# One change to a five-layer attention kernel on one core: keys placed by transfers into kept block-diagonal tiles

## The chip, the core and the metric

The kernel runs on one core of a Trainium2 chip. A core has five engines that run their own instruction streams and wait for each other by semaphores: PE (TensorE, matrix products; PEld is its weight load), DVE (VectorE), ACT (ScalarE), POOL (GpSimd) and SP (SyncE), whose queue here only issues DMA transfers. PE writes its results to PSUM, all other data lie in SBUF, both with 128 partitions. The metric is the device time of one execution in microseconds. A profile is one execution recorded instruction by instruction.

## The reference, cut

The input x has 128 batches of 64 tokens with 128 channels; ctx is a second such tensor and cond one row of 128 channels per batch. Five residual blocks with attention follow each other, then a mixture of experts. All is float32. One attention with 16 heads of 8 channels, as the first block has it:

```python
mod = silu(t_emb) @ adaln_w + adaln_b
sh_sa, sc_sa, g_sa, sh_ff, sc_ff, g_ff = split(mod, 6)
xm = _ln(x) * (1.0 + sc_sa) + sh_sa
q, k, v = heads(xm @ qkv_w + qkv_b)              # 16 heads of 8
attn = softmax(einsum('bhnd,bhsd->bhns', q, k) * 8 ** -0.5)
x = x + g_sa * (einsum('bhns,bhsd->bhnd', attn, v) @ sa_proj_w + sa_proj_b)
```

The order is: layer L0 with self-attention (L0s), cross-attention to ctx (L0c) and an MLP; L1 with cross-attention (L1c); L2 with self-attention (L2s), cross-attention (L2c) and an MLP; L3 with a gated mixture of three experts.

## The kernel before

The tokens are cut into 16 groups of 512 (8 batches), kept in SBUF as xs[s], four tiles of 128 tokens by 128 channels. Each attention layer runs over the 16 groups; a group in a layer is called a unit here, 80 in all, 32 in the first run (L0s, L0c) and 48 in the second (L1c, L2s, L2c). The order of all instructions is written out by hand; nothing is rescheduled. Each engine executes its own in that order, and SP takes its transfers in that order too: one whose condition isn't met holds up all behind it.

A unit passes through three generators.

- prepare (L378) has eight stages: load ctx (c, L386); statistics of x (L312, L314, then POOL's L321, L322); the normalized xn (L364); transposes and modulation into kv_in and q_in; keys kT (PE L428, ACT L430) and from them kbd (L436); queries qT (L441, L443); values (L451) into vbd (L456, L457).
- scores, turned and weighted (L460 to L520) work on a half of a unit (4 batches): PE computes the scores sc (L470) into the only PSUM tile of that kind, DVE takes the maximum mx (L477) and the difference e (L479), PE transposes it (pp, L495), ACT takes the exponential (eT, L499), PE multiplies by vbd (po, L512), ACT copies to o (L520).
- finish (L522) has four stages: sums of the weights leave o for DRAM, come back as rc, and half of o's rows are moved (L530, L534, L537); reciprocal (L539), out as recs, gates gt in self layers (L278), and recs spread back over the partitions as rb (L541, L546); oT = o times rb on POOL (L549); projection py (L555) and the addition to x.

kbd is the block-diagonal form of the keys: partition p holds channel p; for each j of 4 there is a copy in which only channels of heads 4g + j are not zero, so that one product of 32 rows gives the scores of four heads apart. Before, POOL makes the four copies by multiplying kT with a column of a mask of ones and zeros.

vbd holds, for a pair of heads, the values in columns 0 to 7 and 8 to 15, and columns of ones at 16 and 17 that give the softmax's sums. The product po therefore has in each block of 32 rows 16 rows of results and two rows of sums, and o has two such halves; finish moves the second half's rows 0 to 15 to rows 16 to 31 of the first.

attend (L563) interleaves: step k handles a half of unit i. In the first half of unit i it calls, after the scores, one transposition and weighted, in this order: finish of unit i-2 (its stage with recs, gt and rb), prepare of unit i+4 (its first: the load of c), prepare of unit i+1 (its kT and kbd), finish of unit i-3 (projection). In the second half stand prepare of i+1 (queries, then values) and finish of unit i-1 (sums, rc, o) and of i-2 (oT). mlp runs over the groups between the layers, layer_3 at the end; both begin with the same statistics.

Of the kernel before, what the change touches and what calls it, by code (L numbers as in the profile page):

```python
# [35 lines left out]
for _name, _n in _VECS:  # L36
# [14 lines left out]
    "L3_xcond_gate_w1": (3, 128), "L3_xcond_gate_w2": (1, 128), "L3_xcond_out_w": (1, 128),  # L51
}
_RAW = [
    "x", "cond_1024", "ctx_1024", *_WTS,
# [5 lines left out]
def tile_kernel(ctx: ExitStack, tc: tile.TileContext, a: dict, out: bass.AP):  # L60
# [17 lines left out]
    nc.scalar.dma_start(vec_rows, a["vecs"])  # L78
    mask = const([P, 4], "mask")
    nc.scalar.dma_start(mask, a["mask"])  # L80

    w = {}

    def load_weights(prefix, pool=cp):
        for name, (k, n) in _WTS.items():
            if name.startswith(prefix):
                t = pool.tile([P, k, n], F32, tag=name, name=name)
                src = a[name]
                if len(src.shape) == 3:
                    src = src.rearrange("e c n -> (e c) n")  # L90
                nc.sync.dma_start(t, src.rearrange("(k p) n -> p k n", p=P))
                w[name] = t
# [26 lines left out]
    ident = const([P, P], "ident")  # L119
    make_identity(nc, ident)  # L120
    nhalf = const([P, TT], "nhalf")
    G.memset(nhalf, -0.5)
# [45 lines left out]
    ]  # L168

    def clear(t):  # L170
        G.memset(t, 0.0)
        G.memset(t[0:L, :, :, 16:17], 1.0)
        G.memset(t[L:P, :, :, 17:18], 1.0)
# [5 lines left out]
    scT = const([P, P], "scT")  # L179
    mods = {}  # L180

    def col(name, i=0):
        r = _ROW[name] + i
        return vec[:, r : r + 1]
# [20 lines left out]
    def folded_column(wp, bp, bv, i):  # L205
        pb = mm("pb")
        T.matmul(pb[:, 0:1], w[wp][:, 0], col(bv, i), start=True, stop=True)
        t = const([P, 1], "pb_" + wp)
        V.tensor_add(t, pb[:, 0:1], col(bp))
        proj_bias[wp] = t  # L210
# [3 lines left out]
    def gate_table(wmod, wp, i=2, bias=None):  # L214

        table = dp.tile([P, 2, P], F32, tag="gate_" + wp, name="gate_" + wp)
        rows = const([P, 2, P], "gate_rows")
        gb = const([P, P], "gate_bias")
        V.tensor_scalar_mul(gb, mods[wmod][:, i, :], proj_bias[wp] if bias is None else bias)

        def second():
            pg = mm("pg")
            for q, src in enumerate((mods[wmod][:, i, :], gb)):
                T.transpose(pg[:, ts(q, P)], src, ident)
            V.tensor_copy(rows, pg[:, 0 : 2 * P].rearrange("p (i c) -> p i c", i=2))
            nc.sync.dma_start(table, rows)
            gates[wp] = table

        return second

    def folded_row(wp, bp, bv):
        bvs = const([P, P], "bvs")
        V.tensor_copy(bvs, col(bv, 1).broadcast_to([P, P]))

        def second():
            pb = mm("pb")
            T.matmul(pb[:, :P], bvs, w[wp][:, 0], start=True, stop=True)
            V.tensor_add(row_bias[bp], row_bias[bp], pb[:, :P])
            proj_bias[wp] = row_bias[bp]

        return second

    def condition():
        pc = mm("pc")
        T.transpose(pc[:, :P], cond, ident)
        V.tensor_copy(condT, pc[:, :P])
        S.activation(scT, pc[:, :P], AF.Silu)
        pv = mm("pv")
        T.transpose(pv[:, :_NVEC], vec_rows, ident[:_NVEC, :_NVEC])
        V.tensor_copy(vec, pv[:, :_NVEC])  # L250
        V.tensor_scalar_add(vec1, vec, 1.0)

# [20 lines left out]
    def gate_tile(pool, s, wp):  # L273

        gt = pool.tile([P, TT, 2, P], F32, tag="gt", name="gt")
        for h in range(2):
            r = gates[wp].rearrange("(s t h) i c -> s h t (i c)", t=TT, h=2)[s, h]
            nc.sync.dma_start(  # L278
                gt[ts(h, L)].rearrange("p t i c -> p t (i c)"),
                r.unsqueeze(0).broadcast_to([L, TT, 2 * P]),  # L280
            )
        return gt
# [23 lines left out]

    x_mv = const([P, NST, TT, 2], "x_mv")

    def stats(pool, src, mv):
        st = pool.tile([P, TT, 6], F32, tag="st", name="st")  # L310
        for t in range(TT):
            V.bn_stats(st[:, t, :], src[:, t, :])  # L312
        for t in range(TT):
            V.bn_aggr(mv[:, t, :], st[:, t, :])  # L314

# [4 lines left out]
    def power(rs, mv, eps):  # L320
        G.tensor_scalar(rs, mv[:, :, 1], eps, 1.0, ALU.add, ALU.mult)  # L321
        G.tensor_tensor(rs, rs, nhalf, ALU.pow)  # L322
        return rs

    def stats_of(pool, src, eps):
        mv = pool.tile([P, TT, 2], F32, tag="mv", name="mv")
        stats(pool, src, mv)
        return mv, inv_std(pool, mv, eps)
# [30 lines left out]
    def normed_by_pool(pool, src, mv, rs, tag, engine=G):  # L359
        nmu = pool.tile([P, TT], F32, tag="nmu" + tag, name="nmu")  # L360
        G.tensor_scalar(nmu, mv[:, :, 0], -1.0, 0.0, ALU.mult, ALU.add)
        xn = pool.tile([P, TT, P], F32, tag=tag, name=tag)
        for t in range(TT):
            engine.tensor_scalar(  # L364
                xn[:, t, :], src[:, t, :], nmu[:, t : t + 1], rs[:, t : t + 1], ALU.add, ALU.mult
            )
        return xn
# [5 lines left out]

    turn = [0]

    ctxT = dp.tile([NST, P, NT], F32, tag="ctxT", name="ctxT")

    def prepare(pools, at):  # L378
# [54 lines left out]
        vbd = vbds[i]  # L433
        kbd = pool.tile([P, 4, NB, L], F32, tag="kbd", name="kbd")
        for j in range(4):
            (V if at.get("first") else G).tensor_scalar(  # L436
                kbd[:, j], by_batch(kT), mask[:, j : j + 1], 1.0, ALU.mult, ALU.mult
            )
        yield
# [15 lines left out]
        pv4 = pvv.rearrange("p b (i d) -> p b i d", d=HD)  # L455
        S.copy(vbd[0:L, :, :, 0:HD], pv4[0:L])  # L456
        S.copy(vbd[L:P, :, :, HD : 2 * HD], pv4[L:P])  # L457
        at["vbd"] = vbd
# [63 lines left out]
    def finish(pools, at):  # L522
# [5 lines left out]
        sums = dp.tile([16, NT], F32, tag="sums", name="sums", bufs=2)  # L528
        for j in range(2):
            nc.sync.dma_start(  # L530
                sums.rearrange("(g i j) t -> j g i t", i=2, j=2)[j], o[16 + j : P : 32, :, :]
            )
        rc = pool.tile([P, L], F32, tag="rc", name="rc")
        nc.sync.dma_start(rc, sums.rearrange("h (c t) -> (h c) t", t=L))  # L534

        for g in range(4):
            nc.sync.dma_start(o[32 * g + 16 : 32 * g + 32, 0, :], o[32 * g : 32 * g + 16, 1, :])  # L537
        yield
# [6 lines left out]
        rb = pool.tile([P, NT], F32, tag="rb", name="rb", bufs=1)  # L545
        nc.sync.dma_start(rb, recs.unsqueeze(1).broadcast_to([16, HD, NT]))  # L546
        yield
# [69 lines left out]
    def attention_of(s, layer):  # L617
        if layer[2] == "s":
            wmod, wqkv, bqkv, wp = {
                "L0s": ("L0_xcond_adaln_w", "L0_xcond_qkv_w", "L0_xcond_qkv_b", "L0_xcond_sa_proj_w"),  # L620
                "L2s": ("L2_xcond_W_mod", "L2_xcond_W_qkv", "L2_xcond_b_qkv", "L2_xcond_W_proj"),
            }[layer]
            m = w[wqkv][:, 0]
            return dict(
                s=s, layer=layer, wmod=wmod, wp=wp, wq=m[:, 0:P], bq=col(bqkv, 0),
                wk=m[:, P : 2 * P], bk=col(bqkv, 1), wv=m[:, 2 * P : 3 * P],
            )
# [12 lines left out]
        return dict(  # L640
            s=s, layer=layer, wp=wp, wq=w[wq][:, 0], bq=col(bq), wk=m[:, 0:P], bk=col(bkv, 0),
            wv=m[:, P : 2 * P],
# [12 lines left out]
    def measure_context(s):  # L655
        pool = pools[0]
        mv = pool.tile([P, TT, 2], F32, tag="mvc", name="mvc")
        stats(pool, measured[s], mv)
        load_context(s + 2)
        nmu = pool.tile([P, TT], F32, tag="nmuc", name="nmuc")  # L660
        G.tensor_scalar(nmu, mv[:, :, 0], -1.0, 0.0, ALU.mult, ALU.add)
        rs = ctx_rs[:, s]
        for i, eps in enumerate(ctx_eps):
            G.tensor_scalar(rs[:, i], mv[:, :, 1], eps, 1.0, ALU.add, ALU.mult)
        G.tensor_tensor(rs, rs, nhalf.unsqueeze(1).broadcast_to([P, 2, TT]), ALU.pow)
        G.tensor_tensor(ctx_nb[:, s], nmu.unsqueeze(1).broadcast_to([P, 2, TT]), rs, ALU.mult)

    def mlp(wmod, w1, b1, w2, b2, beside, mv_out=None, by_token=False):
# [52 lines left out]
        def leave(d):  # L721
# [4 lines left out]
            if mv_out is not None:  # L726
                stats(pool, xs[d["s"]], mv_out[:, d["s"]])

# [453 lines left out]
    def stages():  # L1182
# [42 lines left out]
        ahead_1(0, 1, 2, 3)  # L1225
        condition()
        ahead_1(0, 0)
        first_mods[0]()
# [14 lines left out]
        n = last + 2 + len(heads_0)  # L1243
        for f in steps_1[6:-n]:
            f()
        for s in range(2):
            heads_0[3 + s] = lambda s=s, f=heads_0[3 + s]: (f(), load_context(s))
# [69 lines left out]
```

## Time and profile before

| what | before |
|---|---|
| median of 3 runs | 1629.09 us (1629.08 to 1633.11) |
| profiled execution, span | 1629.3 us |
| mean granted clock of PE | 0.995 |
| first run of 32 attention units | up to about 400 us |
| MLP of L0 | about 400 to 550 us |
| second run of 48 attention units | about 550 to 1130 us |
| MLP of L2, then L3 | about 1130 to 1629 us |
| POOL on kbd (L436) | 212.7 us, 316 instructions, mean 692 ns |
| DVE on statistics (L312, of x) | 110.5 us, 512 instructions, mean 278 ns |
| DVE on L314 (into mv) | 40.4 us, 448 instructions, mean 152 ns |
| DVE on mx and e (L477, L479) | 366.5 and 366.6 us, 160 each, mean 2291 ns |
| transfers on SP's queue | 108.53 MB, 25.8% of 16 engines |

The page gives each engine's busy time, then the chain: the work that ended last, followed back step by step to what released it. An engine with much idle time that is rarely on the chain can be made lighter or heavier without changing the span, as long as no wait grows out of it. In the chain and the timelines a row starts with its start and its duration in us; "x32" means 32 instructions run together. SPq is SP's queue issuing a transfer; the duration there is that of the issue, not of the transfer.

### The profile page before, as it was taken

What the parts mean: (1) busy time and instruction counts of PE and PEld (TensorE: products, weight loads), DVE (VectorE), ACT (ScalarE), POOL (GpSimd) and SP (SyncE); (2) the same over time, 40 slices, a digit from 0 to 9 for tenths busy, and PEclk for the clock granted to TensorE, in tenths of its full rate; (3) what the DMA queues carried; (4) which work ended last, traced back from release to release, by engine and by line L of the source; (5) the groups of instructions that cost most, each with busy time, mean ns of one, the idle gap of its engine ahead of it and who ended that gap; (6) DMA issues with size and microseconds to landing.
All of it is one profiled execution on the core that took longest, in us unless ns stands there. A gap on an engine that the chain in (4) does not pass through costs nothing.

```text
span 1629.3 us, 64936 instructions
## 1 busy us (share of the span) xinstructions
PE 1578.3 (97%) x27842; PEld 1090.4 (67%) x27842; DVE 1295.3 (79%) x2430; ACT 1036.9 (64%) x1710; POOL 1074.1 (66%) x1786
## 2 busy tenths in 40 slices
PE   6999999998999899999999999998999999999998
PEld 4677767776544467767777777776777666666665
DVE  7999989999566688899999999997454567666666
ACT  5788767776433687787888888886334544444443
POOL 6678776775888789987778877665876333333322
PEclk9999999999999999999999999999999999999999
DMA  7334443322112022211333532222433111111100
GB/s 209 83 82 98 107 119 87 94 80 74 49 33 63 16 60 62 61 52 45 89 91 82 123 90 61 74 56 60 118 91 78 30 40 36 40 33 35 34 11 20
DMA packets 146782, 112.71 MB, mean 69 GB/s; under 512 B 36357, under 2 KB 125247, under 8 KB 146495
## 3 DMA queue, kind: packets, MB, share of 16 engines
q1 hardware_dynamic: 146288, 108.53, 25.8%
q8 instruction: 219, 3.59, 0.9%
q14 instruction: 68, 0.56, 0.1%
q10 hardware_dynamic: 207, 0.03, 0.0%
HBM read 83.99 MB, written 14.02 MB: 60 GB/s over the span
## 4 chain that ended last, share of the span: by engine, by line
PE 80%; DVE 12%; ACT 3%; POOL 2%; DMA 1%; issue 1%; SPq 0%; POOLq 0%; DVEq 0%
PE sc L470 9%; PE pp L495 8%; PE ph L685 7%; PE po L512 7%; PE ph L1072 6%; PE ph L1073 6%; DVE mx L477 5%; DVE e L479 5%; PE po L1103 5%; PE psT L334 5%; PE pk L428 4%; PE py L555 4%; PE py L701 4%; PE py L691 3%; PE pq L441 3%; PE pvv L451 3%
## 5 line engine op out<-in xcount | busy, mean ns | idle before, releaser
L499 ACT ACTIVATE eT<-pp 128x1024 f32<-128x1024 f32 x320 | 329.8, 1031 | 163.2 <-PE pp L495 163.0
L477 DVE TENSOR_REDUCE mx<-sc 128x32 f32<-128x2048 f32 x160 | 366.5, 2291 | 60.2 <-PE sc L470 60.2
L479 DVE TENSOR_TENSOR e<-sc,mx 128x2048 f32<-128x2048 f32 x160 | 366.6, 2291 | 5.4
L495 PEld LDWEIGHTS pp<-ident,e 64*128 64x128 f32 x5120 | 184.9, 139 | 141.0 <-ACT eT L499 45.3
L495 PE MATMUL pp<-ident,e 64*128 64x64 f32 x5120 | 228.7, 229 | 7.1 <-DVE e L479 4.7
L436 POOL TENSOR_SCALAR kbd<-kT,mask 128x512 f32<-128x512 f32 x316 | 212.7, 692 | 30.8 <-ACT kT L430 28.3
L364 POOL TENSOR_SCALAR xn<-x,nmu,rs 128x128 f32<-128x128 f32 x508 | 223.9, 456 | 13.3
L549 POOL TENSOR_TENSOR oT<-o,rb 128x512 f32<-128x512 f32 x80 | 102.1, 1277 | 162.8 <-DMA rb<-recs 60.1
L470 PE MATMUL sc<-kbd,qT 32*64 32x256 f32 x5120 | 181.0, 390 | 17.0 <-DVE e L479 15.2
L686 ACT ACTIVATE h<-ph,vec 128x512 f32<-128x512 f32 x128 | 87.4, 688 | 150.1 <-PE ph L685 149.9
L512 PE MATMUL po<-eT,vbd 128*32 128x64 f32 x10240 | 178.9, 222 | 0.9 <-issue 0.8
L1079 ACT ACTIVATE h<-h 128x512 f32<-128x512 f32 x112 | 70.6, 630 | 148.1 <-DVE h L1075 129.2
L512 PEld LDWEIGHTS po<-eT,vbd 128*32 128x32 f32 x10240 | 152.4, 110 | 13.7 <-DVE st L312 1.5
L322 POOL TENSOR_TENSOR rs<-rs,nhalf 128x4 f32<-128x4 f32 x128 | 130.3, 1018 | 10.7
L470 PEld LDWEIGHTS sc<-kbd,qT 32*64 32x64 f32 x5120 | 98.1, 132 | 53.9 <-issue 19.6
L1075 DVE TENSOR_TENSOR h<-ph,ab 128x512 f32<-128x512 f32 x112 | 76.9, 687 | 56.3 <-PE ph L1073 56.2
L312 DVE BATCH_NORM_STATS2 st<-x 128x6 f32<-128x128 f32 x512 | 110.5, 278 | 0.6
L1108 DVE SCALAR_TENSOR_TENSOR acc<-po,pr,acc 128x128 f32<-128x128 f32 x192 | 67.2, 350 | 44.1 <-PE po L1103 39.6
L1072 PE MATMUL ph<-nx,w 128*128 128x512 f32 x192 | 99.9, 602 | 0.0
L520 ACT COPY o<-po 128x512 f32<-128x512 f32 x160 | 95.7, 598 | 5.5 <-PE po L512 4.1
L1073 PE MATMUL ph<-u,w_ev 128*128 128x512 f32 x192 | 98.0, 592 | 0.0
L1103 PEld LDWEIGHTS po<-w_2o,h 128*128 128x128 f32 x768 | 92.1, 192 | 8.7 <-issue 8.4
(261 smaller groups left out, 2841.2 us busy)
## 6 DMA issues: line engine op xcount, KB each, us to landing
rb<-recs SPq DMA_DIRECT2D x80, 256.0 KB
c<-in_ctx_dram SPq DMA_DIRECT2D x64, 256.0 KB
o<-o SPq DMA_DIRECT2D x320, 32.0 KB
gt<-gate_L_xcond_sa_proj_w SPq DMA_DIRECT2D x32, 256.0 KB
gt<-gate_L_xcond_W_proj SPq DMA_DIRECT2D x32, 256.0 KB
gt<-gate_L_xcond_W_mlp SPq DMA_DIRECT2D x32, 256.0 KB
x<-in_x_dram SPq DMA_DIRECT2D x16, 256.0 KB
ctxT<-cm SPq DMA_DIRECT2D x16, 256.0 KB
```

What stands on the lines that cost most here:

```text
L322: G.tensor_tensor(rs, rs, nhalf, ALU.pow)
L364: engine.tensor_scalar(xn[:, t, :], src[:, t, :], nmu[:, t : t + 1], rs[:, t : t + 1], ALU.add, ALU.mult)
L436: (V if at.get("first") else G).tensor_scalar(kbd[:, j], by_batch(kT), mask[:, j : j + 1], 1.0, ALU.mult, ALU.mult)
L470: T.matmul(sc[ts(h, L), g, ts(t2, 256)], qT[ts(g, 32), ts(b, L)], kbd[ts(g, 32), :, b, :], start=True, stop=True,)
L477: V.tensor_reduce(mx, sc.rearrange("p g (m k) -> p (g m) k", k=L), AX.X, ALU.max)
L479: V.tensor_tensor(e, sc.rearrange("p g (m k) -> p (g m) k", k=L), mx.unsqueeze(2).broadcast_to([P, 32, L]), ALU.subtract,)
L495: T.transpose(pp[:, h, ts(4 * g2 + 2 * i + t2, L)], e6[ts(h, L), 2 * gg + g2, t2, i], ident[ts(h, L), ts(h, L)],)
L499: S.activation(eT[:, gg], pp, AF.Exp, scale=HD ** -0.5)
L512: T.matmul(po[ts(g, 32), i, ts(2 * t2 + h, L)], at["vbd"][:, 4 * u + 2 * t2 + h, 2 * g + i, :], e7[:, g // 2, h, g % 2, i, t2, :], start=T ...
L1072: T.matmul(ps, wn, d["nx"], start=True, stop=False)
L1073: T.matmul(ps, we, d["u"], start=False, stop=True)
L1103: T.matmul(po[:, ex, :], d[q][:, ts(t, P)], k3["w_2o"][:, q, :], start=r == 0, stop=r == 1)
```

## The change

Five parts belong together.

1. kbd becomes two kept tiles, kbds[0] and kbds[1], used in turn. The first two units still fill theirs by the mask, which writes the zeros. From the third on, four transfers on SP's queue (spread) copy 32 rows of 2 KB each from kT to the rows of kbd that aren't zero. For that, the rows of one j have to be p = j, j + 4, ...: the channels of q and k are put in the order (g d j), by reordering the columns of the weights once (reorder; the first on DVE at the start, the others on POOL in the first run) and the biases (vecp).
2. vbd writes the values into even columns; the sums' columns are 1 and 17. All results of po then lie in even rows. One transfer moves the second half into the odd rows (before four), one takes the sums out (before two). rb is filled by two transfers (before one). Projection weights are loaded in that row order, two transfers each, and the value biases follow (vecv).
3. The gates table is stored so that one transfer with rows of 4 KB loads a unit's gates (before two with rows of 1 KB).
4. Statistics take two tiles per call, interleaved, so that the even and odd results of bn_stats are those of the two tiles; bn_aggr goes, and POOL divides the sum of squares by 128.
5. The mask comes from the identity by one DVE reduction, not from DRAM.

```diff
+    kbds = [
+        Places.ak.tile([P, 4, NB, L], F32, tag=f"kbd{i}", name=f"kbd{i}", bufs=1) for i in range(2)
+    ]
     def clear(t):
         G.memset(t, 0.0)
-        G.memset(t[0:L, :, :, 16:17], 1.0)
+        G.memset(t[0:L, :, :, 1:2], 1.0)
         G.memset(t[L:P, :, :, 17:18], 1.0)
...
+    def reorder(engine, name, n):
+        for i in range(n):
+            t = const([P, P], "gate_bias")
+            cols = w[name][:, 0, ts(i, P)]
+            engine.tensor_copy(t.rearrange("p (g d j) -> p g d j", d=HD, j=4), by_element(cols))
+            engine.tensor_copy(cols, t)
...
+        r = gates[wp].rearrange("(s h t) i c -> s h (t i c)", t=TT, h=2)[s]
+        nc.sync.dma_start(
+            gt.rearrange("p t i c -> p (t i c)"),
+            r.unsqueeze(1).broadcast_to([2, L, TT * 2 * P]),
+        )
...
-        for t in range(TT):
-            V.bn_stats(st[:, t, :], src[:, t, :])
-        for t in range(TT):
-            V.bn_aggr(mv[:, t, :], st[:, t, :])
+    def stats(src, mv):
+        for i in range(2):
+            V.bn_stats(mv[:, i, :], src[:, ts(i, 2), :].rearrange("p t c -> p c t"))
...
-        G.tensor_scalar(rs, mv[:, :, 1], eps, 1.0, ALU.add, ALU.mult)
+        G.tensor_scalar(rs, squares(mv), 1.0 / P, eps, ALU.mult, ALU.add)
...
+    def spread(kbd, kT):
+        for j in range(4):
+            nc.sync.dma_start(kbd[j:P:4, j].rearrange("p b l -> p (b l)"), kT[j:P:4, :])
...
-        kbd = pool.tile([P, 4, NB, L], F32, tag="kbd", name="kbd")
-        for j in range(4):
-            (V if at.get("first") else G).tensor_scalar(
-                kbd[:, j], by_batch(kT), mask[:, j : j + 1], 1.0, ALU.mult, ALU.mult
-            )
+        kbd = kbds[i]
+        if turn[0] <= 2:
+            for j in range(4):
+                (V if at.get("first") else G).tensor_scalar(
+                    kbd[:, j], by_batch(kT), mask[:, j : j + 1], 1.0, ALU.mult, ALU.mult
+                )
+        else:
+            spread(kbd, kT)
...
-        S.copy(vbd[0:L, :, :, 0:HD], pv4[0:L])
-        S.copy(vbd[L:P, :, :, HD : 2 * HD], pv4[L:P])
+        S.copy(vbd[0:L, :, :, 0 : 2 * HD : 2], pv4[0:L])
+        S.copy(vbd[L:P, :, :, 2 * HD : 4 * HD : 2], pv4[L:P])
...
-        for j in range(2):
-            nc.sync.dma_start(
-                sums.rearrange("(g i j) t -> j g i t", i=2, j=2)[j], o[16 + j : P : 32, :, :]
-            )
+        nc.sync.dma_start(sums.rearrange("(m i) t -> m i t", i=2), o[1:P:16, :, :])
...
-        for g in range(4):
-            nc.sync.dma_start(o[32 * g + 16 : 32 * g + 32, 0, :], o[32 * g : 32 * g + 16, 1, :])
+        nc.sync.dma_start(o[1:P:2, 0, :], o[0:P:2, 1, :])
...
-        nc.sync.dma_start(rb, recs.unsqueeze(1).broadcast_to([16, HD, NT]))
+        for i in range(2):
+            r = recs.rearrange("(m i) t -> i m t", i=2)[i]
+            nc.sync.dma_start(rb[i:P:2, :], r.unsqueeze(1).broadcast_to([8, HD, NT]))
...
+        reorder(V, "L0_xcond_qkv_w", 2)
```

The last line stands in stages before the first unit's statistics.

## Prediction

> **What bounds the kernel now.** I read the page's busy times, its chain, then one steady period of the chain, the timeline of the same microseconds, and last SP's own rows.
>
> ```profile
> PE 1578.3 (97%) x27842; PEld 1090.4 (67%) x27842; DVE 1295.3 (79%) x2430; ACT 1036.9 (64%) x1710; POOL 1074.1 (66%) x1786
> ...
> PE 80%; DVE 12%; ACT 3%; POOL 2%; DMA 1%; issue 1%; SPq 0%; POOLq 0%; DVEq 0%
> ```
>
> PE is nearly always busy and carries 80% of the chain. POOL, which the change relieves, carries 2%. One attention unit (16 per layer, five layers, 80 in all) in layer L2s:
>
> ```profile
> 792.98 1.12 PE sc L470 x32
> 794.10 0.64 PE pp L495 x16
> 794.74 1.03 PE po L512 x64
> 795.77 1.05 PE pk L428 x2
> 796.83 0.92 PE py L555 x8
> 797.74 0.64 PE pp L495 x16
> 798.38 0.59 PE psT L334 x4
> 798.97 1.13 PE sc L470 x32
> 800.10 0.02 issue
> 800.13 2.30 DVE mx L477
> 802.43 0.02 issue
> 802.45 2.30 DVE e L479
> ```
>
> A unit is two halves. In the first PE alone is full (5.99 us from score to score); in the second sc, mx, e follow one another through the single PSUM tile (5.92 us). Together 11.92 us, and 12.01 in L0c and L2c, 12.27 in L1c (starts of mx in the timelines). There is no slack that a lighter POOL or DVE could use.
>
> ```profile
> 798.53 2.70 POOL L436 TENSOR_SCALAR kbd<-kT,mask 128x512 f32<-128x512 f32 x4
> 798.73 0.54 DVE L539 RECIPROCAL rc<-rc 128x64 f32<-128x64 f32 x1
> ...
> 799.30 0.33 SPq L541 DMA_DIRECT2D recs<-rc  x1
> ```
>
> This is the place to watch. POOL finishes kbd of the next unit at 801.23; its first scores run at 804.89, so today 3.7 us are spare. In the changed kernel those keys are moved by four DMAs that stand in SP's queue behind recs, (gt), rb and (c). SP waits in order, so they inherit every wait ahead of them.
>
> ```profile
> 653.50 0.33 SPq L541 DMA_DIRECT2D recs<-rc  x1
> 655.00 0.56 SPq L546 DMA_DIRECT2D rb<-recs  x1
> 655.61 0.58 SPq L386 DMA_DIRECT2D c<-in_ctx_dram  x1
> ```
>
> rb cannot issue before recs has landed: 1.50 us after recs was issued. Prices of a transfer between SBUF rows, and of a landing:
>
> ```profile
> L537 SPq DMA_DIRECT2D o<-o x320: 507/587/1974, 46.2 to 1145.0; - x160
> ...
> L534 SPq EVENT_SEMAPHORE  x80: 17/1297/2703, 44.5 to 1141.4; - x80
> ```
>
> The issue of an o row move takes 0.59 us of SP; SP then waits 1.30 us (median) for sums to land. The trace's semaphore events give the landing after the end of the issue: o rows 1.37 us, recs 1.14, rb 3.32, c 3.88 (medians).
>
> **The change part by part.**
>
> *Removed from POOL and DVE.* 78 units lose 4 x 0.691 us on POOL (216 us). Statistics go from 4 x 0.276 + 4 x 0.149 = 1.70 us to two calls of twice the length, about 2 x 0.5. In the period above bn_stats sits in DVE's wait for sc (792.75 to 793.9), in layer 3 PE is 100% busy between 1300 and 1400 us. Worth 0. Weight reorders on POOL are 16 copies of about 0.46 us (the xn row), 7 us, hidden by what POOL gives up. If DVE's or POOL's cover were the bound after all, the gain would be some 0.7 us a unit; that is rival 4.
>
> *ACT and the loads.* vbd's copies write every second element. Nearest row: 0.58 us each, plain. If that doubled (bound: 1.2 us more a unit), ACT, busy 151 of 185 us between 725 and 910, has 2.2 us a unit left, and vbd is read only a half later: 0. The five projection weights load in two transfers each; SP's loads end at 33.9 us now, so about 36.5. Behind them stand the first keys, of the third unit: 36.5 + 2.5 + 1.4 = 40.4, before its scores (mx at 44.6): 0.
>
> *SP's count.* A self unit had sums 2, rc, o 4, recs, gt 2, rb = 11 issues; now sums, rc, o, recs, gt, rb 2, keys 4 = 11. Sums, o and gt save 0.6 + 1.9 + 0.65 us of issue, but sums, rc and o stand behind the keys, after the point that matters. gt falls into the wait for recs. So nothing saved helps the keys, while rb's second issue delays them.
>
> *The new loop.* First scores of unit i, mx, e, reciprocal (DVE takes it after e), recs, rb, keys of i+1, first scores of i+1. Steps, in us:
> 1. scores' start to recs' issue: 799.30 - 792.98 = 6.32.
> 2. recs to rb: 1.50.
> 3. two rb issues at 0.56 + 0.04 = 1.20 (a half-sized one, bounds 0.33 to 0.56, taken like the whole). In cross layers also c, 0.62.
> 4. four keys at 0.59 + 0.04: 2.52. They are 32 rows of 2 KB; nearest row the o move, 16 rows of 2 KB, 0.59. Bounds 0.33 (recs, 128 rows of 256 B) and 0.71 (mean of the o moves).
> 5. landing of the last. Empty queues: 1.37. But rb and c fill the same engines: rb2 ends its issue at 2.70 and lands 3.32 later, 6.0; c ends at 3.3 and lands at 7.2. Keys issued last at 5.22 (self) land at 6.6 to 6.8, at 5.84 (cross) at 7.2 to 7.7. I take 6.7 and 7.5 counted from recs; bounds 6.6 and 8.3 (means in place of medians).
> 6. 0.1 for the semaphore.
>
> Medians: self 6.32 + 6.7 + 0.1 = 13.1, cross 13.9. Now the tails: of the o moves one in four lands later than 2.15 and one in ten issues longer than 1.25. Such hold-ups of about 1.5 us come every 10 us or so in the events between 787 and 850 us, and a loop without slack meets one in about half its turns: +0.7. So 13.8 and 14.6.
>
> The loop closes where a unit has both a finishing one two before it and one after it: i = 2 to 30 of the first 32 units, 2 to 46 of the other 48, 74 turns. By what stands ahead of the keys:
> - 20 with gt alone (self): 13.8 - 11.92 = 1.9, 38 us.
> - 12 with gt and c: 14.7 - 12.0 = 2.7, 32 us.
> - 20 with c in L0c and L2c: 14.6 - 12.01 = 2.6, 52 us.
> - 10 with c in L1c: 14.6 - 12.27 = 2.3, 23 us.
> - 12 with neither: 13.7 - 12.0 = 1.7, 20 us.
> Sum 165 us. While PE waits there, nothing behind sc can run on it: pp, po, pk, py of the same half all queue behind, and ACT and POOL wait for those.
>
> *Start.* DVE now reorders the first q and k weights before the first statistics. By the semaphore events those weights land at 6.4 us; statistics began at 4.38. Four copies at 0.29 (the condT copy) and 0.2 for waits end at about 7.8, two statistics at 8.8 instead of 5.53, and the chain of the start runs through them: +3.
>
> Profiled execution 1629.3 + 165 + 3 = 1797; the median of the runs is 1629.09, so nothing is to be added.
>
> [...]
> [...]
>
> ```profile
> 403.20:405.50 2.30, 0.01 (x2) 0.04 (x2) 2.14 (x1) 1.02 (x1) 0.12 (x1) 1.00 0.37 119
> ...
> 406.10:409.40 3.30, 3.30 (x74) 3.07 (x71) 0.36 (x1) 1.61 (x2) 3.20 (x6) 0.50 0.17 35
> ```
>
> After a PE gap of 2.34 us the granted clock is 0.50 for 3.3 us; after one of 1.85 us (at 227) it stays 1.00. [...]
>
> **Rivals.**
> 1. *The clock falls too.* Stalls of 1.9 to 2.7 us lie around the two gaps above. At 0.50 the scores take 2.0 instead of 1.12 us (2.01 at 15.80, at the start), which lengthens the loop by 0.9; the rest of the loss falls into the stall, which then shrinks, so at most every other turn is hit: up to 37 x 0.9 = 33. 1797 + 33 = 1830, up to 1865 with slow landings. For: the row above. Against: gaps of 2.02 (1278) and 1.85 left the clock alone.
> 2. *The issue is cheap.* Keys issue at 0.33 like recs and hold-ups hide: 13.8 - 1.04 - 0.4 per turn, 74 x 1.44 = 107 less, 1690. For: recs and rc have as many descriptors as rows and are short. Against: every transfer of 2 KB rows shown takes 0.5 or more.
> 3. *Keys hidden after all* (not slower). If keys landed within 5.6 us of recs, which is what a period of 12 allows, the stall is nil: 1629 + 3 = 1632. For: 3.7 us of slack now. Against: 1.50 + 1.20 + 4 x 0.37 + 1.37 = 5.55 with the cheapest issue and no queue, and c on top; it decides only if issues fall to 0.33 and nothing holds them.
> 4. *Relief pays.* With keys hidden, L1c falling to 11.92 (16 x 0.35), L0c and L2c to 11.92 (30 x 0.09) and the seam after L0s (POOL's chain, 14.1 us in one unit) give 10 us less: 1622. Against: those periods are PE and ACT rows, not POOL.
>
> **How the numbers follow.** Forecast 1797, its own range 1740 to 1830: 0.61. Clock 0.15, cheap issue 0.15, hidden 0.05, relief 0.04. The range 1715 to 1865 takes in half of the cheap-issue case and nearly all of the clock's; outside it lie about 0.17. What cannot be told from no change is 0.3%, 5 us: slower 0.91 (0.61 + 0.15 + 0.15), same 0.05 (rival 3), faster 0.04 (rival 4).
>
> **What would show it.** In the profile after: PE's largest wait is sc for a DMA into kbd, once per unit, 1.2 to 2.7 us; first mx to first mx 13.5 to 15 us in all attention layers, cross above self; SP's keys begin right behind rb or c, 0.6 us each; POOL's busy time falls by some 200 us, DVE's by some 60, for nothing; MLP and layer 3 are as long as before. If sc waits for DVE's e as now, the loop isn't closed and the forecast falls. If the clock row shows many stretches of 0.50, rival 1 holds.

## The result, and the profile after

The changed kernel takes 2165.93 us (median; 2162.89 to 2171.29) against 1631.10 us before in the same series: 1.3285 times as long, 95% interval 1.3267 to 1.3303. The forecast was 1797 with a range up to 1865. Direction and place were right, the size was not: 535 us were lost instead of 168.

The page of the changed kernel (engines' busy times, then the granted clock in 40 slices, then the chain by engine and by line):

```profile
PE 1691.9 (78%) x27844; PEld 1167.1 (54%) x27844; DVE 1242.8 (57%) x1575; ACT 1043.6 (48%) x1710; POOL 869.5 (40%) x1490
...
PEclk9778777899999999998787887799999898999999
...
PE 46%; DMA 25%; SPq 8%; ACT 7%; issue 5%; DVE 5%; POOL 3%; POOLq 0%; DVEq 0%; ACTq 0%
DMA kbd<-kT 16%; PE sc L542 7%; SPq L443 6%; PE pp L567 5%; PE ph L1142 5%; PE po L584 4%; PE ph L1143 4%; DMA gt<-gate_L_xcond_W_mlp 4%; PE po L1173 4%; PE pk L497 3%; PE ph L755 3%; ACT eT L571 3%; PE py L625 3%; PE py L761 3%; DMA rb<-recs 2%
```

PE was busy 97% of the span and is now at 78%, though its matmuls take 114 us more: the clock row falls to 7 and 8 in both attention runs (mean 0.894; 460 us of the span at half clock against 15 before). POOL lost 204.6 us of work and DVE 52.5, as the diff promises, and little of either stood on the chain before: POOL's kbd carried 9.7 us of it, DVE's statistics 5.4. Transfers, 1% of the chain before, are now 25%, and SP's issues 8%.

Who waits for them (waits of the changed kernel: total us, times, longest):

```profile
POOL oT L619 <- DMA rb<-recs: 497.6, 51, 19.1
...
PE sc L542 <- DMA kbd<-kT: 391.8, 72, 11.5
...
DVE y L781 <- DMA gt<-gate_L_xcond_W_mlp: 110.9, 15, 13.5
```

The middle row is the wait that was forecast: scores for the keys' transfers, once per turn (72 times). Forecast were 1.2 to 2.7 us each; the mean is 5.4 and the longest 11.5. The last row was not forecast at all: in the second MLP the result waits for its gates.

Cut at the first mx of the first and of the last unit of each run, the 536 us between the two profiled spans (1629.3 and 2165.2) are: the start +2.1, the first 32 units +213, the MLP of L0 -1.9, the other 48 units +266, the second MLP and L3 +57. Now the attention units by what stands ahead of the keys in SP's queue of the changed kernel. Mean turn in us (first mx to first mx), in the two kernels and in the experiments that come next:

| ahead of the keys | turns | forecast | before | after | gates in two | gates in two, c behind the keys | gates in two, keys ahead of recs | gates in two, keys by POOL |
|---|---|---|---|---|---|---|---|---|
| recs, gt, rb | 20 | 13.8 | 11.94 | 22.94 | 15.04 | 15.03 | 12.42 | 11.95 |
| recs, gt, rb, c | 12 | 14.7 | 12.27 | 23.81 | 15.72 | 14.91 | 12.57 | 12.11 |
| recs, rb, c (L0c, L2c) | 20 | 14.6 | 12.01 | 14.94 | 15.03 | 14.38 | 12.73 | 12.09 |
| recs, rb, c (L1c) | 10 | 14.6 | 12.26 | 15.19 | 15.42 | 14.20 | 12.58 | 12.25 |
| recs, rb | 12 | 13.7 | 12.11 | 14.81 | 14.62 | 14.29 | 12.61 | 12.13 |

The five groups fall apart into two. Turns without gates are 0.3 to 1.1 us above the forecast. The 32 turns with gates are 9 us above it. One of those, in L2s, in the timeline of the changed kernel (start, duration, engine, line, what; in brackets the idle time before, and who ended it; rows of other work left out):

```profile
1052.13 2.02 PE L542 MATMUL sc<-kbd,qT 32*64 32x256 f32 x32 [11.47 <-DMA kbd<-kT]
...
1059.34 0.33 SPq L609 DMA_DIRECT2D recs<-rc  x1
...
1059.71 0.58 SPq L333 DMA_DIRECT2D gt<-gate_L_xcond_W_proj  x1
...
1062.51 1.25 SPq L616 DMA_DIRECT2D rb<-recs  x2
...
1063.87 3.37 SPq L443 DMA_DIRECT2D kbd<-kT  x4
```

The scores have waited 11.47 us and then run at half clock (2.02 us instead of 1.12). SP is not the trouble: the keys are all issued 7.9 us after recs. The trace's semaphore events show that a landing is reported in parts, up to 16 for one transfer; the page counts 16 DMA engines, and I take each part for the share of one of them, called a path here. The partial completions of the same transfers, in us after the end of the issue:

```
issue    transfer  completions  when they came
1059.71  gt         3           0.42, 11.95, 12.34
1062.51  rb         9           0.42, six from 1.92 to 2.37, 9.74, 10.15
1063.19  rb         9           0.43, six from 2.13 to 2.71, 9.78, 10.20
1063.87  kbd       16           fourteen from 1.24 to 2.29, 9.35, 9.76
1064.42  kbd       16           fourteen from 1.18 to 3.02, 8.91, 9.31
1065.06  kbd       16           fourteen from 1.15 to 2.60, 8.47, 8.87
1065.69  kbd       16           fourteen from 1.15 to 1.33, 7.06, 7.45
1067.28  sums       9           0.41, six from 1.15 to 1.31, 6.60, 6.99
```

Here the turn can be read off. The gates' transfer has 3 completions where both transfers of before had 16, and it lands 12.3 us after its issue. Of every transfer listed behind it, all completions but two arrive by 3.02 us, and two are late, 6.6 us or more; their last parts come at 1072.6, 1073.3, 1074.0, 1074.2, 1074.3, 1074.5, 1074.7 and 1074.9, one after another in the order of issue. The trace's packets agree: the gates' 128 of 4 KB, about 0.16 us each, run two at a time from 1061.1 to 1072.2. So I read that two of the 16 paths are occupied, and that what has a share on them waits. (Neither events nor packets name the path; that the late parts share the gates' two is inferred from their number and their order.) Over all 32 units with gates the landing takes 11.9 to 13.8 us (median 12.6) for 512 KB; before, each of two transfers of 256 KB took 3.5 us.

### The profile page after: what moved, and what is told of

Its sections match the earlier page's. It is cut to its first block, busy times and chain, and to the rows that moved or that the text cites. A ratio compares the mean times of both kernels' runs of the same rounds, so it can differ in the third digit from the quotient of the medians.

```text
span 2165.2 us, 63830 instructions
## 1 busy us (share of the span) xinstructions
PE 1691.9 (78%) x27844; PEld 1167.1 (54%) x27844; DVE 1242.8 (57%) x1575; ACT 1043.6 (48%) x1710; POOL 869.5 (40%) x1490
## 3 DMA queue, kind: packets, MB, share of 16 engines
q1 hardware_dynamic: 136920, 128.98, 18.6%
## 4 chain that ended last, share of the span: by engine, by line
PE 46%; DMA 25%; SPq 8%; ACT 7%; issue 5%; DVE 5%; POOL 3%; POOLq 0%; DVEq 0%; ACTq 0%
DMA kbd<-kT 16%; PE sc L542 7%; SPq L443 6%; PE pp L567 5%; PE ph L1142 5%; PE po L584 4%; PE ph L1143 4%; DMA gt<-gate_L_xcond_W_mlp 4%; PE po L1173 4%; PE pk L497 3%; PE ph L755 3%; ACT eT L571 3%; PE py L625 3%; PE py L761 3%; DMA rb<-recs 2%
## 5 line engine op out<-in xcount | busy, mean ns | idle before, releaser
L542 PE MATMUL sc<-kbd,qT 32*64 32x256 f32 x5120 | 217.9, 455 | 399.4 <-DMA kbd<-kT 391.8
L542 PEld LDWEIGHTS sc<-kbd,qT 32*64 32x64 f32 x5120 | 114.4, 152 | 444.2 <-issue 398.2
L567 PEld LDWEIGHTS pp<-ident,e 64*128 64x128 f32 x5120 | 202.4, 151 | 156.9 <-issue 67.0
L567 PE MATMUL pp<-ident,e 64*128 64x64 f32 x5120 | 248.7, 243 | 7.0 <-DVE e L551 4.5
L427 POOL TENSOR_SCALAR xn<-x,nmu,rs 128x128 f32<-128x128 f32 x508 | 223.7, 453 | 13.2
L584 PE MATMUL po<-eT,vbd 128*32 128x64 f32 x10240 | 208.7, 244 | 0.0
L584 PEld LDWEIGHTS po<-eT,vbd 128*32 128x32 f32 x10240 | 180.9, 126 | 14.7 <-DVE mv L368 1.5
L631 POOL TENSOR_TENSOR x<-x,y 128x512 f32<-128x512 f32 x32 | 40.7, 1273 | 154.3 <-DVE y L630 135.3
L1173 PE MATMUL po<-w_2o,h 128*128 128x128 f32 x768 | 95.8, 275 | 0.0
```

The source lines that it names most:

```text
L427: engine.tensor_scalar(xn[:, t, :], src[:, t, :], nmu[:, t : t + 1], rs[:, t : t + 1], ALU.add, ALU.mult)
L542: T.matmul(sc[ts(h, L), g, ts(t2, 256)], qT[ts(g, 32), ts(b, L)], kbd[ts(g, 32), :, b, :], start=True, stop=True,)
L567: T.transpose(pp[:, h, ts(4 * g2 + 2 * i + t2, L)], e6[ts(h, L), 2 * gg + g2, t2, i], ident[ts(h, L), ts(h, L)],)
L584: T.matmul(po[ts(g, 32), i, ts(2 * t2 + h, L)], at["vbd"][:, 4 * u + 2 * t2 + h, 2 * g + i, :], e7[:, g // 2, h, g % 2, i, t2, :], start=T ...
L1173: T.matmul(po[:, ex, :], d[q][:, ts(t, P)], k3["w_2o"][:, q, :], start=r == 0, stop=r == 1)
```

## The experiments

**Gates by two transfers again.** The theory from the table above (A): the gates' single transfer costs the excess in the 32 turns and the MLP. The rival (C): the keys' transfers alone make turns of 23 us. In this kernel everything is as in the changed one, with one loader replaced:

```diff
-        r = gates[wp].rearrange("(s h t) i c -> s h (t i c)", t=TT, h=2)[s]
-        nc.sync.dma_start(gt.rearrange("p t i c -> p (t i c)"),
-            r.unsqueeze(1).broadcast_to([2, L, TT * 2 * P]))
+        for h in range(2):
+            r = gates[wp].rearrange("(s h t) i c -> s h (t i c)", t=TT, h=2)[s, h]
+            nc.sync.dma_start(gt[ts(h, L)].rearrange("p t i c -> p (t i c)"),
+                r.unsqueeze(0).broadcast_to([L, TT * 2 * P]))
```

> The changed kernel with each unit's gates loaded by two transfers of 64 rows of 4 KB in place of one of 2 x 64 rows; same bytes, same rows, same table. Theory A (the one transfer runs on few DMA engines, 3 completions seen where others show 16, and what is queued behind it lands with it): gates land in 3 to 4 us, not 12.5; turns in self layers fall from 23 to 13.5 to 15 us as in the cross layers, the end of the second MLP loses its 57 us; 1780 to 1840. Rival C (the keys' transfers themselves are slow, or rows of 4 KB read from DRAM are): self turns stay above 20, above 2050.

Measured: 1850.46 us, ratio 1.1357 (1.1316 to 1.1398). So 315 of the 535 us go with the gates, although the rows of 4 KB stay and a transfer more is issued. The gates now have 16 completions and land after 3.3 us. The wait for keys falls to less than half (waits of this kernel):

```profile
POOL oT L620 <- DMA rb<-recs: 240.9, 40, 11.1
PE sc L543 <- DMA kbd<-kT: 179.8, 71, 5.4
```

In the turns, 20 x 7.9 and 12 x 8.1 make 255 us, and the part behind the last unit's first mx is 512 us long again instead of 567. C falls. A misses its upper end by 10 us; that remainder belongs to the keys, below.

**Gates in two transfers, each for both halves.** One transfer or two, row length, bytes per transfer and the outermost dimension of 2 all differ between the kernels above. Here the count is two, the bytes are 256 KB each as before, but each still goes to both halves:

```diff
-        nc.sync.dma_start(gt.rearrange("p t i c -> p (t i c)"),
-            r.unsqueeze(1).broadcast_to([2, L, TT * 2 * P]))
+        for q in range(2):
+            nc.sync.dma_start(gt[:, ts(q, 2)].rearrange("p t i c -> p (t i c)"),
+                r[:, ts(q, 2)].rearrange("h t k -> h (t k)").unsqueeze(1).broadcast_to([2, L, 4 * P]))
```

> The changed kernel with the gates in two transfers, each of 2 x 64 rows of 2 KB (two tiles of 128 tokens), instead of one of 2 x 64 rows of 4 KB. The same count and the same bytes as in e1, but e1 cut between the two halves of 64 rows, so that a transfer's outermost dimension was 64; here it is 2 as in the changed kernel. Theory A (the outermost dimension of 2 leaves two engines): again about 3 completions per transfer, gates land 12 us or more after issue, 2140 to 2200. Rival (one long transfer, or rows of 4 KB, are slow): as e1, 1840 to 1870.

Measured: 2161.10 us, ratio 1.3257 (1.3219 to 1.3294), the loss of the changed kernel; 3 completions per transfer again. So it is neither the count nor the bytes of one transfer: a source of [2, 64, ...] landed with 3 completions here and in the changed kernel, one of [64, ...] with 16 in the kernel before and in the one with gates in two. The counts of the changed kernel's other transfers go with the first number of the pattern too: rb and sums, whose patterns begin with 8, have 9 completions, one of them 0.4 us after the issue like the gates' first; the keys' 32 rows have 16. In the kernel before, sums began with 4 and had 5. What makes the counts so is not shown.

**The gates' part alone.** The kernel before, with its keys by POOL, and only the gates' table and their single transfer taken over (the diff's part 3).

```diff
-            nc.sync.dma_start(table, rows)
+            for h in range(2):
+                nc.sync.dma_start(
+                    table.rearrange("(s h t) i c -> h s t (i c)", t=TT, h=2)[h],
+                    rows[h:P:2].rearrange("p i c -> p (i c)"))
...
-        for h in range(2):
-            r = gates[wp].rearrange("(s t h) i c -> s h t (i c)", t=TT, h=2)[s, h]
...
+        r = gates[wp].rearrange("(s h t) i c -> s h (t i c)", t=TT, h=2)[s]
+        nc.sync.dma_start(gt.rearrange("p t i c -> p (t i c)"),
+            r.unsqueeze(1).broadcast_to([2, L, TT * 2 * P]))
```

> The kernel before with one part of the change: the gates' table in the new order and one transfer per unit. Keys by POOL, everything else as before. Theory A: 256 KB on each of two engines are 12 us a unit, and rb, o and sums queue behind them on these two; self turns of 15 to 18 us without any keys on the queue, cross layers 12.0, the second MLP 50 to 60 us longer; 1780 to 1900. Rival (only keys behind the gates hurt, as PE waits for nothing else there): 1630 to 1700, all of it in the second MLP.

Measured: 1884.01 us, ratio 1.1557 (1.1529 to 1.1585): 254 us without any key on the queue. The waits of this kernel name the other way that the slow transfer takes:

```profile
PEld py L558 <- POOL oT L552: 178.7, 45, 7.6
...
DVE rc L542 <- DMA rc<-sums: 112.0, 34, 5.9
DVE y L714 <- DMA gt<-gate_L_xcond_W_mlp: 91.9, 13, 12.9
```

sums and rb of self units land late, so the projection comes late on PE, and in the second MLP the gates themselves are late. Gates alone cost 254 and keys alone 220 (next), together 535. The 61 us above the sum I take for what keys lose by standing behind gates; a later run agrees (one transfer, keys ahead of recs).

**Keys by POOL, all else changed.** The gates in two, and the mask's products for every unit, not just the first two:

```diff
-        if turn[0] <= 2:
+        if True:
```

> As e1, and kbd is filled by POOL with the mask in all units; no keys on SP's queue. Everything else of the change stays (even rows, fewer transfers of sums and halves, statistics of two tiles, reordered weights). Theory B (with the gates mended, what is left comes from the keys' place on SP's queue alone): 1627 to 1640, of which 3 for the start. Rival (values in every second column, rb in two or the new statistics cost too): above 1650. Rival (the lighter DVE pays): below 1624.

Measured: 1630.84 us, ratio 1.0006 (0.9996 to 1.0017). The even rows of o, the fewer transfers of sums and halves, the two transfers of rb, the joined statistics and the reordered weights together gain nothing and cost nothing that can be told (POOL has its old work again here, DVE is 53 us lighter); the keys' transfers cost the whole 220 us between this kernel and the first one. The one thing visible is the start (DVE's timeline of this kernel):

```profile
7.06 0.23 DVE L284 COPY L_xcond_qkv_w<-gate_bias 128x128 f32<-128x128 f32 x1
7.20 0.75 DVE L369 BATCH_NORM_STATS2 mv<-x 128x6 f32<-128x256 f32 x2
...
20.33 2.29 DVE L550 TENSOR_REDUCE mx<-sc 128x32 f32<-128x2048 f32 x1 [2.25 <-PE sc L543]
```

Statistics begin behind the last copy, at 7.20 instead of 4.38, and the first mx at 20.33 instead of 17.91.

**The same, with the copies behind the first statistics.**

```diff
-        reorder(V, "L0_xcond_qkv_w", 2)
         ahead_1(0, 0)
+        reorder(V, "L0_xcond_qkv_w", 2)
```

> The kernel after with gates by two transfers and keys always by POOL, as before, and DVE's reordering of the first q and k weights moved behind the first unit's statistics. The theory that these four copies are what the start costs: in the kernel with keys by POOL the statistics of x ran at 7.20 instead of 4.38 us and the first mx at 20.33 instead of 17.91; with the copies moved, statistics at about 4.7, copies from 6.2 to 7.3 inside DVE's wait for POOL's nmu, first mx at 17.8 to 18.4, and the time about 2 us below that kernel's: 1627 to 1630, ratio 0.998 to 1.000. The rival, that something else of the start is late (the three transposes of the vectors, the mask from the identity): first mx stays at 20 or above.

Measured: 1628.72 us, ratio 0.9991 (0.9981 to 1.0001). DVE's timeline of this kernel:

```profile
4.67 0.76 DVE L369 BATCH_NORM_STATS2 mv<-x 128x6 f32<-128x256 f32 x2
...
17.92 2.29 DVE L550 TENSOR_REDUCE mx<-sc 128x32 f32<-128x2048 f32 x1 [1.36 <-PE sc L543]
```

The first mx is back at 17.92: the four copies were the start's 2.4 us. Against the kernel before the interval includes 1, so even this, the change without its two costly transfers and without its late start, is no version that beats it measurably.

**Keys ahead of recs.** If the loop of the prediction is what makes the turns long, then keys that are issued before recs leave the loop. With gates in two:

```diff
+                go(prep, i + 1)
                 go(fin, i - 2)
                 go(prep, i + 4)
-                go(prep, i + 1)
                 go(fin, i - 3)
```

> As e1, but in the first half of a unit the stage with kT and the keys is called ahead of the finishing stage with recs, gt and rb and of the load of c, so the keys stand ahead of them on SP's queue. Theory B (order on the queue): keys are issued from about 4.6 us after the first scores, land by 9 to 10, before the next first scores at 12; turns of 11.9 to 12.5, no wait of scores for keys, 1625 to 1650. Rival (a transfer from kT is too slow or meets too much traffic wherever it stands): scores still wait, above 1700.

Measured: 1665.07 us, ratio 1.0214 (1.0197 to 1.0232). The order in SP's queue is worth 185 of the 220 us; the rival falls. The upper end was missed by 15. What is left has another place (waits of this kernel; the same row had 14.5 us in 21 waits before):

```profile
PEld py L626 <- POOL oT L620: 74.6, 67, 3.8
```

recs and rb now stand behind the four keys, so oT is later and PE's projection waits. That this wait makes up the remaining 35 us is read from the waits, not shown by a run.

**The same order, with the gates' single transfer.**

> The changed kernel with the order of e4 but the gates still in one transfer. Theory A with B: 256 KB on each of two engines take 12.4 us, and with that engine's share of rb, keys and the rest some 16 us a unit, which then bounds the self layers although the keys are ahead: turns of 15 to 18 there, cross layers at 12 to 12.5, the second MLP still 50 to 60 us longer; 1790 to 1900. If only the keys' place behind the gates mattered (order alone): 1640 to 1700.

Measured: 1923.15 us, ratio 1.18 (1.1755 to 1.1845), 23 above the upper end. So the order doesn't cure the gates: keys are ahead of them now, but rb and sums are not, and turns with gates still take 18.0 and 19.2 us, while those without are at 12.3 to 13.2. Against the same order with gates in two (1665.07) the single transfer costs 258 us, about the 254 of the gates alone: with the keys ahead, the 61 us are gone.

**c behind the keys.** One term of the forecast's sum by itself, with gates in two:

```diff
                 go(fin, i - 2)
-                go(prep, i + 4)
                 go(prep, i + 1)
+                go(prep, i + 4)
                 go(fin, i - 3)
```

> The kernel after with gates by two transfers (1850 us, cross turns with c 15.0, without c 14.6), and the load of c issued behind the keys instead of ahead of them. The theory of the prediction's sum, that every issue ahead of the keys lengthens the loop by its own length: 42 turns with c, each shorter by 0.6 to 0.8, 25 to 34 us in all, 1815 to 1826. The rival, that turns are set by hold-ups and stretches of half clock that come whatever stands in the queue: 1840 to 1860, turns with c at 14.9 to 15.1 as they were.

Measured: 1811.20 us, ratio 1.1110 (1.1093 to 1.1127), some 40 us less by the two ratios, a little more than expected. Turns with c are 0.65, 0.81 and 1.22 shorter, 0.83 on the mean of the 42. Of the turns without c, the 20 with gates are 0.01 shorter and the 12 others 0.33, 0.13 on the mean. The difference, 0.7, is near the 0.62 on record for one issue; the groups scatter too much to say more than that an issue ahead of the keys lengthens the turn by about its own length. The wait for keys falls by 43 us:

```profile
PE sc L543 <- DMA kbd<-kT: 136.7, 62, 4.0
```

**Keys issued by ACT.** Gates in two, keys' four transfers on ACT's queue, which stands behind none of SP's waits:

```diff
-            nc.sync.dma_start(kbd[j:P:4, j].rearrange("p b l -> p (b l)"), kT[j:P:4, :])
+            nc.scalar.dma_start(kbd[j:P:4, j].rearrange("p b l -> p (b l)"), kT[j:P:4, :])
```

> As e1 (gates in two by halves, calls in the changed kernel's order), but the keys' four transfers are issued by ACT right after kT instead of by SP. Theory B (the place on SP's queue is the price): keys land by 9 us after the first scores; no wait of scores for keys; what is left is ACT's time, four issues of about 0.55 us a unit on an engine that has 2.2 us a unit free: turns of 12.0 to 13, 1635 to 1710. Rival (the transfers are too slow wherever they are issued): above 1800.

Measured: 1761.90 us, ratio 1.0811 (1.0790 to 1.0833): between both expectations, a miss for both. The timeline of this kernel shows why:

```profile
799.98 2.41 ACTq L444 DMA_DIRECT2D kbd<-kT  x4
...
801.42 1.12 PE L543 MATMUL sc<-kbd,qT 32*64 32x256 f32 x32
...
802.44 1.02 ACT L572 ACTIVATE eT<-pp 128x1024 f32<-128x1024 f32 x1 [2.48 <-DMA kbd<-kT]
803.51 0.71 PE L568 MATMUL pp<-ident,e 64*128 64x64 f32 x16 [0.97 <-ACT eT L572]
```

The scores no longer wait. But the four issues hold ACT for 2.4 us, the exponential stands behind them (187 us of ACT's waits in all, put down to the keys), and PE waits for that. The price of an issue moved from one queue to another engine's work.

**Keys ahead of recs, projection later.** To take away the wait for oT, the projection of unit i-3 was moved from the first half of a unit into the second:

```diff
                 go(prep, i + 1)
                 go(fin, i - 2)
                 go(prep, i + 4)
-                go(fin, i - 3)
+                if i - 3 == n - 1:
+                    go(fin, i - 3)
             else:
+                if i - 3 < n - 1:
+                    go(fin, i - 3)
                 go(prep, i + 1)
```

> As e4 (keys ahead of recs, gt and rb), and the projection py of unit i-3 is computed in the second half of unit i instead of the first, 6 us later. If the 35 us that e4 still costs are rb landing late behind the keys, so that oT is late and PE waits for it at py: 1625 to 1645. If they are something else (traffic on the DMA engines, ACT, kT late for SP): 1655 to 1675, as e4.

Measured: 1695.65 us, ratio 1.0398 (1.0379 to 1.0418), a miss on both sides. The wait for oT is gone, but the halves are out of balance: the second takes 6.6 us of PE's work, and the first waits for DVE's e instead (timeline of this kernel):

```profile
795.76 1.12 PE L543 MATMUL sc<-kbd,qT 32*64 32x256 f32 x32
...
801.66 1.12 PE L543 MATMUL sc<-kbd,qT 32*64 32x256 f32 x32 [0.82 <-DVE e L552]
...
808.26 1.12 PE L543 MATMUL sc<-kbd,qT 32*64 32x256 f32 x32
```

5.90 and 6.60 us make 12.50. The edit changed two things, the wait and the balance, and so leaves open what the 35 us above were.

## Where the prediction was right and where it failed

**The step that failed** is in "SP's count": "gt falls into the wait for recs. So nothing saved helps the keys". It counted the gates' transfer as one issue of SP (0.65 us saved) and took for granted that it lands as its two forerunners did. Its landing was never costed, in step 5 either, where only rb and c "fill the same engines". It lands in 12.6 us instead of 3.5, and two parts of each transfer behind it come late with it: 315 us of the miss of 369. The other 54 are the allowance for hold-ups, below. What the runs then priced stood in the diff: the pattern on the DRAM side begins with 2, where before it began with 64. The change's other new patterns (rb and sums with 8, keys with 32) were equally unexamined, and those did no such harm (ratio 1.0006 with the new rb and sums and keys by POOL; with gates in two the last keys landed 1.63 us after their issue).

**The loop was right**: its direction, its place, its length without hold-ups. A turn of the kernel with gates in two, in the timeline:

```profile
427.16 1.12 PE L543 MATMUL sc<-kbd,qT 32*64 32x256 f32 x32 [2.50 <-DMA kbd<-kT]
...
433.48 0.33 SPq L610 DMA_DIRECT2D recs<-rc  x1
...
435.00 1.31 SPq L617 DMA_DIRECT2D rb<-recs  x2
...
436.41 0.39 SPq L456 DMA_DIRECT2D c<-in_ctx_dram  x1
...
436.89 2.43 SPq L444 DMA_DIRECT2D kbd<-kT  x4
...
440.81 1.12 PE L543 MATMUL sc<-kbd,qT 32*64 32x256 f32 x32 [1.56 <-DMA kbd<-kT]
```

Scores to recs 6.32 (forecast 6.32), recs to rb 1.52 (1.50), rb to the keys 1.89 (1.20 + 0.62), the keys' issue 2.43 (2.52), the last landed 1.35 after it, scores 0.14 later. This turn has 13.65 us; the forecast for such a turn without hold-ups was 13.9.

**The allowance for hold-ups was too small.** Over the 74 turns of that kernel the means against the terms on record are: recs to rb 2.07 against 1.50, the keys' issue 3.03 against 2.52, landed to mx 1.61 against 1.32 (0.1 and the scores' 1.22). Together 1.4 us a turn, and 0.1 at rb, where 0.7 was allowed. That is the 220 us of the keys against the forecast 165. The 0.1 for the semaphore was an estimate without a row behind it; in the changed kernel the 72 scores that waited for keys began 0.14 after the landing (median). The 0.29 at the scores is in the main rival 1, the clock: the scores of this kernel took 197.3 us in all instead of 181.0, 16 us more, within its bound of 33. In the changed kernel they took 217.9, 37 us more, and the term from landed to mx is 2.3 in the turns with gates. So rival 1 was no alternative but a part of the whole; what half clock cost in PE's other work is not isolated.

The keys' landing was costed right: the last keys of the kernel with gates in two landed 1.63 after the end of their issue on the mean, 0.05 above the term that the forecast used, and the loss came from the issues and from recs.

**The rest.** That relief of DVE is worth nothing was right: ratio 1.0006, L1c 12.25 against 12.26, with DVE 53 us lighter and POOL as before. Relief of POOL stands in no run by itself. But in the kernel with keys ahead of recs no scores wait for keys and POOL is 200 us lighter, and its undisturbed turns are about what they were: 12.26 in L1c, 12.01 in L0c and L2c, 11.87 against 11.92 where gates are loaded. That speaks against rival 4. Rival 3, hidden keys, fell with the result, as scores waited for keys 72 times. The start: +3 forecast, 2.1 measured in the changed kernel and 2.4 in the one with keys by POOL, by the copies named. "MLP and layer 3 are as long as before": right for the first MLP, which loads no gates, wrong by 57 us for the second. Rival 2, cheap issues: falls, keys issue in 0.59 (median).

## What to carry to other kernels

Cost a transfer by its landing and by what stands behind it, not by its issue, and look at the outermost dimension before joining transfers: two transfers over 64 rows, 16 completions and 3.5 us each, became one over 2 x 64 with 3 completions and 12.6 us. A transfer that feeds the bound engine belongs ahead of everything in its queue that waits (185 of 220 us here); moving it to a free queue pays only if the engine that issues it has the time at that place (on ACT four issues held the exponential for 2.4 us, and 132 us of loss stayed). Work taken off DVE (53 us) and, as far as the turns show, off POOL (200 us) was worth nothing here, since little of it stood on the chain, while the means of relief put a wait into every turn.

## What the runs showed of the hardware

*Behind the slow transfer a few parts came late.* In the turn of the changed kernel above, of the keys behind the gates fourteen parts of sixteen landed in 1.2 to 3.0 us and two in 7 to 10, and the scores began at 1074.82, 0.13 after the last part; a mean share of busy DMA engines (18.6% after, 25.8% before) does not show it.

*The hold-ups go with the loading of instructions.* The page of the kernel with gates in two lists it among the DMA queues (packets, MB, share):

```profile
q8 instruction: 219, 3.59, 0.8%
```

219 packets of 16 KB, about 1.1 us each, one every 6 us (median), and as many in the kernel before. In the kernel with gates in two such a packet overlapped 43 of the 80 transfers of recs between issue and landing; 25 of these landed later than 1.8 us after the end of their issue, and none of the other 37. All 49 issues of keys longer than 0.9 us overlapped one too; of the 263 shorter ones 33 did. In the changed kernel's turn above, recs at 1059.34, fifteen completions came by 1.11 and one at 2.79, beside a packet from 1060.2 to 1061.3. This is read from the traces; every kernel here had 219 of them, so it was not tried, and the cause stays unproven.

*The clock.* Scores that ran at half clock (over 1.5 us) by the gap of PE before them, in the kernel with gates in two:

```
gap on PE, us     cases   at half clock
under 2.2         42       1
2.2 to 3.5        23       8
over 3.5          17      12
```

In the changed kernel all 32 gaps over 8 us were followed by it. Longer gaps were followed by half clock more often, and no length in these rows parts the two: a third of the gaps from 2.2 to 3.5 us were, and 5 of the 17 over 3.5 us were not.
